# A two-layer mixture kernel: loads held back behind a run-time branch, a single placed inside a pair, and a sort drawn more slowly

## The chip, the core and the metric

The kernel runs on one core of one Trainium2 chip. Time is device time in microseconds (us), the median of three runs. A core has TensorE (PE in the profile; PEld is its weight load), VectorE (DVE), ScalarE (ACT), GpSimd (POOL) and SyncE (SP). SP issues most loads, POOL the stores of results; all transfers run on the core's 16 DMA engines.

## What is computed

Sixteen samples x of 256 tokens by 256 features pass through two layers, each with a residual. In layer 0 each sample goes through one of eight experts, the one with the largest value in `cond_8`; in layer 1 through its two largest, weighted, and through a shared one.

```python
def _L0_cond_ref(x, opcode_onehot, W_up, b_up, W_gate, b_gate, W_down, b_down):
    expert = jnp.argmax(opcode_onehot, axis=-1)
    wu, bu = (W_up[expert], b_up[expert])
    ...
    hidden = jax.nn.silu(up) * gate
    return jnp.einsum('bsh,bdh->bsd', hidden, wd) + bd[:, None, :]

def _L1_cond_ref(x, router_logits, skill_gate, skill_up, skill_down, shared_gate, shared_up, shared_down):
    rw = jax.nn.softmax(router_logits.astype(jnp.float32), axis=-1)
    w, sel = jax.lax.top_k(rw, 2)
    ...
    # out = sum over the two experts of w * (gelu(x @ gate) * (x @ up)) @ down
    return out + _gemma_mlp(x, shared_gate, shared_up, shared_down)

x = x + _L0_cond_ref(x, cond_8, ...)
x = x + _L1_cond_ref(x, cond_8, ...)
```

The hidden width is 512 in layer 0 and 1024 in layer 1. Everything is float32.

## The kernel before

**Units.** Work is cut into units. A `Single` takes one sample through one expert. A `Pair` takes two samples that use the same expert and saves one eighth of the products by Strassen's scheme (Winograd's form): seven block products (`STEPS`) in place of eight. The sums that this needs are made by POOL for the weights (`sums_q`, `sums_d`, lines 411 to 414) and by DVE for the activations (`sums_b`, lines 404 to 406). To find pairs, the kernel sorts the samples by expert at run time: `order_of_work`, once for layer 0 (16 entries) and once for layer 1 (32 entries: sample and expert for both choices). In layer 1 at least 12 pairs exist whatever the input; the remaining eight entries form 0 to 4 more pairs, and what is then left are singles. That number, `more_i`, is known only at run time.

**Quarters.** The hidden dimension of a unit is cut into quarters (two in layer 0, four in layer 1). For each quarter SP loads a block of gate and up weights (`load_q`, line 342, six buffers "q"), and PE does the ups (line 466 for a pair, 613 for a single) into the PSUM banks X, Y and Q. ACT copies X out (447), DVE combines that copy with Y and Q (451), ACT applies the activation (493) and DVE multiplies (494) and makes the sums for the down products. A single has one DVE operation per quarter, 624 in layer 1 and 632 in layer 0. The down weights come by `load_d` (351) into two buffers "d"; the downs (518 for a pair, into A, B and Y; 643 for a single, into Y) give the result, which DVE finishes (540 on ACT, 551), and POOL adds it to the output in HBM (384).

**Order.** Nothing is scheduled by a compiler: the order of instructions on every engine is the order in which the program emits them. `Line` is a hand-made clock. `main` emits a step and moves the clock (two units for a step of a pair, eight for a quarter of a single), and `later` queues a step for a time. So a pair's seven downs stand between the ups of the next unit, from 18 units after the pair's end, one each 6 units. At each quarter `Line.ahead` issues loads five quarters ahead and POOL's sums three ahead. In layer 0 a single can stand among the quarters of a pair (`among`).

**The second sort.** It is a Python generator, `routing`: the softmax, the second choice and the sort of 32 entries, some 45 small DVE operations; the large ones work on 128x1024. `Line.quarter` draws five steps of it at quarters 2 and 3, and one at each later quarter, so its operations stand in DVE's queue between those of the units:

```python
            for _ in range(5 if self.at < 4 else 1):
                next(routing, None)
```

**The branch.** Every engine reads `more_i` (856) and jumps to one of five bodies (`tc.Switch`, 862). In each body stand a shared pair, the singles that are left (`left`), the additional pairs (`more_pairs[:k]`) and two more shared pairs. With this input k is 3: two singles and three pairs. The first instruction of SP in the body is the load of the next quarter:

```python
        left = ones[2 * k :]
        rest = [shared[-NB], *left, *more_pairs[:k], *shared[1 - NB :]]
        quarters[common:] = in_order(rest)[shared[-NB].kp :]
        u, j = quarters[common]
        u.load_q(j)
        run(rest)
```

**Buffers.** `take` hands out the buffers of a ring in turn; "xs" (four of 512 columns) holds a single's samples, "as" (two) its activations in layer 0, "d" (two of 2048 columns) down weights.

Of the kernel before, what the change touches and what calls it, by code (L numbers as in the profile page):

```python
# [1 line left out]

# [5 lines left out]
F32 = mybir.dt.float32  # L8
I32 = mybir.dt.int32
AF = mybir.ActivationFunctionType  # L10
# [4 lines left out]
B, S, D, E = 16, 256, 256, 8  # L15
H0, H1 = 512, 1024
P = 128
KD = D // P
KPS = (H0 // P // 2, H1 // P // 2)
# [7 lines left out]
NB = 3  # L27
N2 = 2 * S
# [30 lines left out]
def kernel(  # L59
# [10 lines left out]
    nc = tc.nc  # L70
# [3 lines left out]
    const = ctx.enter_context(tc.tile_pool(name="const", bufs=1))  # L74
# [6 lines left out]

    RINGS = {
        "q": (6, QB), "s": (5, QB), "d": (2, 4 * KPS[1] * P), "ds": (2, 4 * KPS[1] * P),
        "c": (2, 8 * S), "bt": (7, 7 * S), "xt": (2, 7 * S), "xs": (4, KD * S), "cp": (6, N2),
        "as": (2, N2), "dz": (5, S), "ys": (3, 4 * S), "z": (1, 4 * S), "bq": (4, 4),
    }
    BANKS = {"X": 2, "Y": 2, "Q": 2, "A": 1, "B": 1}
    rings = {
        tag: [const.tile([P, width], F32, name=f"{tag}{i}") for i in range(n)]
        for tag, (n, width) in RINGS.items()  # L90
    }
    rings |= {
        tag: [ps.tile([P, N2], F32, name=f"{tag}{i}") for i in range(n)] for tag, n in BANKS.items()
    }
    turns = {tag: list(range(len(ring))) for tag, ring in rings.items()}
    HELD = ("s", "d", "bt", "ys", "cp")

    turns |= {("later", tag): [] for tag in HELD}

    def take(tag, *shape, of=None):  # L100

        i = turns[tag].pop(0)
        if tag not in HELD:
            turns[tag].append(i)
        else:
            assert (tag, of) not in turns
            turns[tag, of] = i
        t = rings[tag][i]
        n = 1
        for d in shape:  # L110
            n *= d
        t = t[:, :n]
        if len(shape) == 1:
            return t
        names = "abcd"[: len(shape)]
        return t.rearrange(
            f"p ({' '.join(names)}) -> p {' '.join(names)}", **dict(zip(names, shape))
        )

    def when_free(tag, f):  # L120

        if turns[tag] and not turns["later", tag]:
            f()
        else:
            turns["later", tag].append(f)

    def give(tag, of):
        turns[tag].append(turns.pop((tag, of)))
        if turns["later", tag]:
            turns["later", tag].pop(0)()  # L130

    def bank(tag):
        return take(tag, N2)
# [21 lines left out]
    num = const.tile([P, NA], F32, name="num")  # L155
# [145 lines left out]
    class Unit:  # L301
# [30 lines left out]
            return v[:, self.at + t : self.at + t + 1]  # L332


        def load_q(self, j, parts=1):
            t = take("q", QB)
            w = (wq0, wq1)[self.layer]
            src = w[bass.ds(self.expert(), 1), j].rearrange("e p f -> (e p) f")
            width = src.shape[1]
            cuts = [0, QW // 2, width] if parts == 2 else [0, width]  # L340
            for lo, hi in zip(cuts, cuts[1:]):
                nc.sync.dma_start(t[:, lo:hi], src[:, lo:hi])
            self.q[j] = t[:, :QW].rearrange("p (m k h) -> p m k h", m=2, k=4)
            self.bq = getattr(self, "bq", {}) | {j: t[:, QW:]}
# [44 lines left out]
                give("ys", self)  # L389

    class Pair(Unit):
        width, last = 2, False


        def sums_x(self):
# [185 lines left out]
        def run(self, line, among):  # L581

            self.start()
            for j in range(self.kp):
                line.quarter(self, j)
                for k in range(6):
                    line.main(UP, lambda j=j, k=k: self.up(j, k))

                line.later(2 * UP, lambda j=j: self.up(j, 6))
                line.later(  # L590
                    3 * UP, lambda j=j: when_free("bt", lambda: self.act(j))
                )
                line.later(6 * UP, lambda j=j: self.act_sums(j))
                for f in among[j] if j < len(among) else ():
                    f()

            first, step = 18, 6 if self.layer else 3
            if self is shared[-2]:
                step = 7
            for k in range(7):  # L600
                line.later(first + step * k, lambda k=k: self.down(k))

    class Single(Unit):
        width = 1

        def up(self, j):

# [29 lines left out]

        def down(self, j):
            if j == 0:
                self.po = bank("A" if self is l0_ones[0] else "Y")  # L640
            for half in range(2):
                for c in range(KD):
                    nc.tensor.matmul(  # L643
                        self.po[:, bass.ts(c, S)],
                        lhsT=self.d[:, 2 * c + half, j, :],
                        rhs=self.acts[j][:, bass.ts(half, S)],
                        start=(j == 0 and half == 0 and c == 0),
                        stop=(j == self.kp - 1 and half == 1),
                        skip_group_check=True,
                    )  # L650
            if self.layer:
                give("cp", (self, j))
            if j < self.kp - 1:
                return
            if self.layer:
                give("d", self)
                ys = take("ys", KD, 1, S, of=self)
                nc.scalar.activation(
                    ys.rearrange("p c t s -> p (c t s)"), self.po, AF.Copy, scale=self.weight(0)
                )  # L660
                self.done(ys)
            else:
                give("s", self)
                for c in range(KD):
                    xv = self.xt[:, c, :]
                    nc.vector.scalar_tensor_tensor(
                        xv, self.po[:, bass.ts(c, S)], self.bd[:, c : c + 1], xv, ALU.add, ALU.add
                    )
                self.done(self.xt.unsqueeze(2))

        def piece(self, line, j):
            line.quarter(self, j)
            if not self.layer:
                self.up(j)
            else:
                line.main(SINGLE_UP, lambda: self.up(j))
            if self.layer:
                line.later(SINGLE_UP, lambda: self.down(j))
# [23 lines left out]
    l0_first = First(next(names), 0, B - 1)  # L702
    l0_pairs = [Pair(next(names), 0, 2 * i) for i in range(NP1)]
    l0_ones = [Single(next(names), 0, 2 * NP1 + i) for i in range(NS1)]
    shared = [Pair(next(names), 1, None, (2 * i, 2 * i + 1)) for i in range(NPR)]
    pairs = [Pair(next(names), 1, 2 * i) for i in range(NP2)]
    more_pairs = [Pair(next(names), 1, 2 * NP2 + 2 * i) for i in range(NS2 // 2)]
# [4 lines left out]
    among = {u: [[] for _ in range(u.kp)] for u in [*units, *more_pairs, *shared]}  # L712
# [6 lines left out]
    def in_order(units):  # L719

        order = []
        for u in units:
            for j in range(u.kp):
                order.append((u, j))
                for p in among[u][j] if u in among else ():
                    one = p.__self__
                    if p == one.ups:
                        order += [(one, i) for i in range(one.kp)]
        return order

    quarters = [(u, j) for u in (l0_first, l0_ones[0]) for j in range(u.kp)]
    quarters += in_order(units)
    Q_AHEAD, S_AHEAD = 5, 3

    class Line:
# [52 lines left out]
        def quarter(self, unit, j):  # L788

            self.at += 1  # L790
            assert quarters[self.at] == (unit, j)
            self.ahead(self.at)
            self.send()
            for _ in range(5 if self.at < 4 else 1):
                next(routing, None)

        def send(self):
# [4 lines left out]
    line = Line()  # L802
# [31 lines left out]
    def run(units):  # L834
        for u in units:
            if u.width == 2:
                u.run(line, among[u])
            else:
                for j in range(u.kp):
                    u.piece(line, j)  # L840

    quarters += in_order(shared[-NB:-NB + 1])
    run(units)
    for _ in routing:
        pass
# [16 lines left out]
    for k in tc.Switch(which, NS2 // 2 + 1):  # L862
        for o, d in entry:
            o.clear()
            o.update({n: v.copy() if isinstance(v, (list, dict)) else v for n, v in d.items()})
        left = ones[2 * k :]
        rest = [shared[-NB], *left, *more_pairs[:k], *shared[1 - NB :]]
        quarters[common:] = in_order(rest)[shared[-NB].kp :]
        u, j = quarters[common]
        u.load_q(j)  # L870
        run(rest)
        line.flush(1 << 30)
        line.send()


# [56 lines left out]
```

## Time and profile before

| what | us |
|---|---|
| median of 3 runs | 1071.12 (1071.01 to 1071.39) |
| the profiled execution | 1071.5 |
| its span | 1069.9 |
| PE busy | 1049.1 (98%) |
| DVE busy | 772.9 (72%) |
| POOL busy | 573.8 (54%) |
| ACT busy | 342.2 (32%) |
| DMA | 136.96 MB, mean 128 GB/s |

The page gives busy times, the span in 40 slices, the chain of work that ended last, and the costliest groups of instructions. A busy PE is not a PE at its peak: matmuls are pipelined and their ends are modelled, so gaps of PE are read from the starts of the groups that follow one another. The mean granted clock of TensorE is 0.995 of full speed. The first matmul stands at 1.60 us and a pair's ups begin at 26.10; the branch lies at 774 to 784 us; the two singles run from 821 to 874, and the additional pairs follow them.

### The profile page before, as it was taken

To read this page: it belongs to the slowest core of one execution; us is meant where nothing else is said; L and a number is where in the kernel's file an instruction comes from. 1 tells how busy PE (TensorE), PEld (TensorE's weight loads), DVE (VectorE), ACT (ScalarE), POOL (GpSimd) and SP (SyncE) were. 2 spreads that over 40 slices of the span, in tenths; PEclk is the share of its full clock that TensorE was granted. 3 is DMA by queue.
4 is the path that set the end of the run, shared out by engine and by line. 5 is a ranking of instruction groups with operands and counts; after the bars stand their busy time and mean duration, and the time that the engine had idled before them with its cause. 6 is when DMAs were issued, how large, how long until landed. Compare 5 with 4: busy or idle time off the path is not lost.

```text
span 1069.9 us, 14169 instructions
## 1 busy us (share of the span) xinstructions
PE 1049.1 (98%) x4786; PEld 910.0 (85%) x4786; DVE 772.9 (72%) x1166; ACT 342.2 (32%) x546; POOL 573.8 (54%) x630
## 2 busy tenths in 40 slices
PE   8999999999999999999999999999979999999998
PEld 6788888888888888888888888888868887888887
DVE  7898776677877787778777777877755128777774
ACT  2222233333333333333333333333323113333331
POOL 2554454956664675477556756664620156664520
PEclk9999999999999999999999999999989999999999
DMA  7555565453453355335534552454344364354222
GB/s 253 188 187 205 194 191 165 178 131 95 110 138 110 88 135 138 92 89 138 138 99 99 138 137 85 113 138 114 87 101 113 88 201 126 101 138 117 50 71 42
DMA packets 48854, 136.96 MB, mean 128 GB/s; under 512 B 4994, under 2 KB 17410, under 8 KB 45570
## 3 DMA queue, kind: packets, MB, share of 16 engines
q1 hardware_dynamic: 33666, 115.22, 33.9%
q0 software_dynamic: 14816, 20.45, 11.0%
q8 instruction: 41, 0.67, 0.3%
q14 instruction: 43, 0.35, 0.1%
q10 hardware_dynamic: 288, 0.26, 0.1%
HBM read 114.95 MB, written 20.97 MB: 127 GB/s over the span
## 4 chain that ended last, share of the span: by engine, by line
PE 85%; DVE 9%; issue 3%; ACT 2%; DMA 1%; SPq 0%; DVEq 0%; ACTq 0%
PE X L466 21%; PE Q L466 14%; PE Y L466 14%; PE A L518 11%; PE B L518 8%; PE Y L518 7%; PE Y L643 3%; DVE c L451 3%; PE X L613 3%; PE Q L613 2%; DVE bt L404 1%; DVE bt L494 1%; ACT c L493 1%; PE Y L613 1%; DVE bt L405 1%
## 5 line engine op out<-in xcount | busy, mean ns | idle before, releaser
L447 ACT ACTIVATE cp<-X 128x512 f32<-128x512 f32 x300 | 178.7, 596 | 524.1 <-PE X L466 522.6
L494 DVE TENSOR_TENSOR bt<-c 128x1024 f32<-128x1024 f32 x92 | 135.6, 1474 | 95.6 <-ACT c L493 95.6
L466 PE MATMUL Q<-xt,s 128*128 128x256 f32 x736 | 191.2, 383 | 7.4 <-DVE c L451 7.4
L466 PE MATMUL Y<-xt,q 128*128 128x256 f32 x736 | 190.4, 381 | 2.0 <-DVE c L451 1.8
L466 PE MATMUL X<-xt,s 128*128 128x256 f32 x736 | 191.1, 382 | 0.0
L466 PEld LDWEIGHTS Q<-xt,s 128*128 128x128 f32 x736 | 140.4, 192 | 28.6 <-issue 6.8
L466 PEld LDWEIGHTS Y<-xt,q 128*128 128x128 f32 x736 | 138.5, 190 | 25.6 <-DVE c L451 7.0
L466 PEld LDWEIGHTS X<-xt,s 128*128 128x128 f32 x736 | 140.5, 192 | 21.2 <-issue 1.3
L451 DVE TENSOR_TENSOR c<-cp,Q 128x512 f32<-128x512 f32 x200 | 135.8, 679 | 26.2 <-ACT cp L447 21.3
L411 POOL TENSOR_TENSOR s<-q 128x256 f32<-128x256 f32 x100 | 93.9, 939 | 107.3 <-PE Q L466 63.0
L384 POOL DMA_DIRECT2D out_dram<-ys x46 | 49.0, 1066 | 184.9 <-DVE ys L551 68.8
L451 DVE TENSOR_TENSOR c<-cp,Y 128x512 f32<-128x512 f32 x200 | 135.6, 678 | 16.6 <-PE X L466 8.5
L414 POOL TENSOR_TENSOR s<-s,q 128x256 f32<-128x256 f32 x100 | 77.4, 774 | 113.0 <-PE Q L466 113.0
L493 ACT ACTIVATE c<-c 128x1024 f32<-128x1024 f32 x92 | 96.8, 1052 | 22.3 <-DVE c L451 22.2
L412 POOL TENSOR_TENSOR s<-s,q 128x256 f32<-128x256 f32 x100 | 98.7, 987 | 8.4 <-PE Y L643 0.7
L404 DVE TENSOR_TENSOR bt<-bt 128x512 f32<-128x512 f32 x104 | 101.5, 976 | 1.0 <-DMA bt<-x_dram 0.9
L413 POOL TENSOR_TENSOR s<-q 128x256 f32<-128x256 f32 x100 | 95.9, 959 | 0.0
L466 PE MATMUL X<-xt,q 128*128 128x256 f32 x368 | 94.5, 379 | 0.9 <-issue 0.9
L518 PE MATMUL Y<-bt,d 128*128 128x256 f32 x400 | 95.1, 379 | 0.0
L518 PE MATMUL B<-bt,ds 128*128 128x256 f32 x400 | 95.1, 379 | 0.0
L518 PE MATMUL A<-bt,ds 128*128 128x256 f32 x400 | 95.1, 379 | 0.0
L518 PEld LDWEIGHTS Y<-bt,d 128*128 128x128 f32 x400 | 76.0, 190 | 10.3
(129 smaller groups left out, 1230.9 us busy)
## 6 DMA issues: line engine op xcount, KB each, us to landing
q<-wq_dram SPq DMA_DIRECT2D x100, 512.0 KB, 3.6
d<-wd_dram SPq DMA_DIRECT2D x25, 1024.0 KB, 6.4
out_dram<-ys POOLq DMA_DIRECT2D x54, 256.0 KB, 4.4
xt<-x1d SPq DMA_DIRECT2D x46, 256.0 KB, 4.8
q<-wq_dram SPq DMA_DIRECT2D x22, 514.0 KB, 3.8
s<-wd_dram SPq DMA_DIRECT2D x8, 513.0 KB, 4.8
d<-wd_dram SPq DMA_DIRECT2D x4, 513.0 KB, 5.7
xs<-x_dram SPq DMA_DIRECT2D x8, 256.0 KB, 3.8
```

Source lines behind the costliest of these rows:

```text
L404: tt(t[:, 4:6, :], t[:, 0:3:2, :], t[:, 2:4, :], ALU.subtract)
L411: tt(s("S1"), a("A21"), a("A22"), ALU.add)
L412: tt(s("S2"), s("S1"), a("A11"), ALU.subtract)
L413: tt(s("nS3"), a("A21"), a("A11"), ALU.subtract)
L414: tt(s("nS4"), s("S2"), a("A12"), ALU.subtract)
L447: nc.scalar.activation(t, self.banks["X", j], AF.Copy)
L451: nc.vector.tensor_tensor(self.c[j][:, block].rearrange("p m s -> p (m s)"), self.copies[n, j], self.banks[tag, j], op,)
L466: nc.tensor.matmul(self.banks[tag, j][:, bass.ts(m, S)], lhsT=self.q[j][:, m, A_AT[a], :] if a in A_AT else self.s[j][:, m, S_AT[a], :], r ...
L493: nc.scalar.activation(u, u, AF.Gelu_apprx_tanh)
L494: nc.vector.tensor_tensor(t[:, 0:4, :], u, v, ALU.mult)
L518: nc.tensor.matmul(d, lhsT=src[:, j, :], rhs=self.acts[j][:, B_AT[b], :], start=OPENS[k] and j == 0, stop=j == self.kp - 1, skip_group_che ...
L613: nc.tensor.matmul(dst[:, bass.ts(half, S)], lhsT=self.q[j][:, m, 2 * half + c, :], rhs=self.xt[:, c, :], start=(c == 0), stop=(c == KD - 1),)
```

## The change

Four edits, all in the program that emits instructions:

1. Behind the branch the first load of SP gets `behind=True`: before it, DVE, POOL and ACT each write one element of the buffer that the load fills, so that the load, and all that SP issues after it, waits for the three writes. They are the first instructions of these three engines in the body.
2. The last of the singles behind the branch is not a unit of its own any more: its quarters stand among the quarters of the first additional pair (the `host`), its ups right behind that pair's ups of the same quarter, its downs into bank A; the first single's downs go to bank B. The downs of the shared pair in front of them start 24 units after its end instead of 18. For this a third buffer "d" is made of a new tile `spare`; before the branch the same tile serves as two of the four "xs" and as both "as" buffers, so that no memory is added.
3. The second sort is drawn with five steps at quarter 2 and two at quarter 3, then one at each.
4. `po_bank`, `first` and the handling of a `partial` in `in_order` are what these need.

```diff
-        "c": (2, 8 * S), "bt": (7, 7 * S), "xt": (2, 7 * S), "xs": (4, KD * S), "cp": (6, N2),
-        "as": (2, N2), "dz": (5, S), "ys": (3, 4 * S), "z": (1, 4 * S), "bq": (4, 4),
+        "c": (2, 8 * S), "bt": (7, 7 * S), "xt": (2, 7 * S), "xs": (2, KD * S), "cp": (6, N2),
+        "as": (0, N2), "dz": (5, S), "ys": (3, 4 * S), "z": (1, 4 * S), "bq": (4, 4),
...
+    spare = const.tile([P, 4 * KPS[1] * P], F32, name="spare")
+    for i, (tag, at) in enumerate((("xs", 2), ("xs", 3), ("as", 0), ("as", 1))):
+        rings[tag].insert(at, spare[:, i * N2 : (i + 1) * N2])
+        turns[tag].append(at)
+    rings["d"].append(spare)
...
-        def load_q(self, j, parts=1):
+        def load_q(self, j, parts=1, behind=False):
+
             t = take("q", QB)
+            if behind:
+                nc.vector.memset(t[:1, 0:1], 0.0)
+                nc.gpsimd.memset(t[:1, 1:2], 0.0)
+                nc.scalar.activation(t[:1, 2:3], num[:1, :1], AF.Copy)
...
-            first, step = 18, 6 if self.layer else 3
+            first, step = self.first, 6 if self.layer else 3
...
-                self.po = bank("A" if self is l0_ones[0] else "Y")
+                self.po = bank(self.po_bank)
...
-        def piece(self, line, j):
+        def piece(self, line, j, among=False):
             line.quarter(self, j)
-            if not self.layer:
+            if among or not self.layer:
                 self.up(j)
...
-            for _ in range(5 if self.at < 4 else 1):
+            for _ in range({2: 5, 3: 2}.get(self.at, 1)):
                 next(routing, None)
...
-        rest = [shared[-NB], *left, *more_pairs[:k], *shared[1 - NB :]]
+        rest = [shared[-NB], *left[:-1], *more_pairs[:k], *shared[1 - NB :]]
+        turns["xs"], turns["d"] = [0, 1], [*turns["d"], 2]
+        if left:
+
+            host = rest[len(left)]
+            for j in range(host.kp):
+                among[host][j].append(partial(left[-1].piece, line, j, among=True))
+            left[-1].po_bank, left[0].po_bank = "A", "B"
+            shared[-NB].first = 24
         quarters[common:] = in_order(rest)[shared[-NB].kp :]
         u, j = quarters[common]
-        u.load_q(j)
+        u.load_q(j, behind=True)
```

More of the change, by code (lines that the diff above doesn't have):

```diff
@@ L1 @@
 from contextlib import ExitStack
+from functools import partial
 import concourse.bass as bass
@@ L391 @@
     class Pair(Unit):
-        width, last = 2, False
+        width, last, first = 2, False, 18
         def sums_x(self):
@@ L603 @@
     class Single(Unit):
-        width = 1
+        width, po_bank = 1, "Y"
         def up(self, j):
@@ L704 @@
     l0_ones = [Single(next(names), 0, 2 * NP1 + i) for i in range(NS1)]
+    l0_ones[0].po_bank = "A"
     shared = [Pair(next(names), 1, None, (2 * i, 2 * i + 1)) for i in range(NPR)]
@@ L725, in in_order @@
                 for p in among[u][j] if u in among else ():
-                    one = p.__self__
-                    if p == one.ups:
+                    one = p.func.__self__ if isinstance(p, partial) else p.__self__
+                    if isinstance(p, partial):
+                        order.append((one, p.args[1]))
+                    elif p == one.ups:
                         order += [(one, i) for i in range(one.kp)]
@@ L873 @@
         line.send()
+        for a in among[rest[len(left)]]:
+            a.clear()
 def kernel(**inputs):
```

## The prediction

> **What bounds the kernel now.** The page comes first: TensorE is busy 98% of the span, and the chain that ended last is 85% PE. Time can therefore only come from PE work, which the change leaves as it is, or from PE's gaps. So I listed PE's waits over 0.3 us in the timeline, then read the branch by its source lines, by short windows and by the chain of waits, and last the DVE rows in front of each gap.
>
> First PE's large gaps, in the timeline (start, duration, row, idle before it and its releaser):
> ```profile
> 33.35 1.13 PE L466 MATMUL Y<-bt,q 128*128 128x256 f32 x4 [2.50 <-DVE as L632]
> 55.33 1.13 PE L466 MATMUL Q<-bt,s 128*128 128x256 f32 x4 [0.84 <-DVE c L451]
> ...
> 785.19 1.13 PE L466 MATMUL Y<-xt,q 128*128 128x256 f32 x4 [1.43 <-DVE c L451]
> 790.56 2.04 PE L466 MATMUL Q<-xt,s 128*128 128x256 f32 x4 [4.24 <-DVE c L451]
> 898.47 1.59 PE L466 MATMUL Q<-xt,s 128*128 128x256 f32 x4 [2.00 <-DVE c L451]
> ```
> They lie in three places: the start, the branch, and the first pair behind two singles. Each releaser is DVE. A x4 group costs 0.86 us (steps of the chain), a x8 group 1.73.
>
> The branch, by source lines: when each engine reads the branch's value (L856) and passes the target's hint (L862):
> ```profile
> L856 SPq TENSOR_LOAD <-more_i x1: 275/275/275, 753.7 to 753.7; - x1
> L856 DVEq TENSOR_LOAD <-more_i x1: 543/543/543, 775.5 to 775.5; - x1
> ...
> L862 SPq BRANCH_PREFETCH_HINT  x1: 55/55/55, 757.6 to 757.6; - x1
> L862 POOLq BRANCH_PREFETCH_HINT  x1: 56/56/56, 762.2 to 762.2; - x1
> L862 PEldq BRANCH_PREFETCH_HINT  x1: 50/50/50, 774.7 to 774.7; - x1
> L862 ACTq BRANCH_PREFETCH_HINT  x1: 50/50/50, 774.7 to 774.7; - x1
> L862 DVEq BRANCH_PREFETCH_HINT  x1: 56/56/56, 784.2 to 784.2; - x1
> ```
> With the jumps (L927: SP 754.2, POOL 759.6, PE 770.8, ACT 772.2, DVE 776.7) the fetch takes 3.4, 2.6, 3.9, 2.5 and, for DVE alone, 7.5 us. The chain of waits shows that PE's gap is this delay:
> ```profile
> 776.78 7.45 issue
> 784.23 0.06 DVEq L862
> ...
> 784.45 1.30 DVE c L451 x2
> ...
> 786.86 2.96 DVE bt L494
> 789.82 0.61 DVE c L451
> ...
> 790.56 2.04 PE Q L466 x4
> ```
> The windows give the reason (us, then busy of PE, PEld, DVE, ACT, POOL, then PEclk, DMA share, GB/s): full DMA engines during DVE's fetch, and a lower clock after it.
> ```profile
> 778.00:780.00 2.00, 2.00 (x11) 1.77 (x10) 0.00 (x0) 0.60 (x1) 0.00 (x0) 1.00 0.97 241
> 785.00:797.00 12.00, 7.57 (x20) 5.92 (x21) 9.91 (x11) 2.63 (x4) 7.39 (x5) 0.72 0.33 77
> ```
> The traffic is q (512 KB, issued 772.35), d (1024 KB, 773.98) and one out_dram write (774.71, landed after 9.3 us; median 4.4).
>
> [...] Here 0.72 on average follows 4.24 us idle, but 2.00 us idle at 898 also cost clock (0.89 over 898 to 914) and 2.50 at 33 did not. [...] L209 beside POOL took 1.75 us against 1.22 alone; the reduce L210 beside POOL took 1.22.
>
> **Part A, loads behind the branch.** SP's first q load now waits for tiny writes by DVE, POOL and ACT, each the first instruction behind its own branch. Behind it on SP queue q, then d (now in a third d buffer, so it no longer waits for PE, and it is held by this wait alone), then loads that PE's pace releases later (783.03 on). In the trace they left between 760 and 774; now all leave at about 780. Their readers: L613 on the first q at 820.5; d for POOL's ds (786.97), which PE reads at 843. 2 MB at the 241 GB/s above lands by 790, so 30 us of cover remain; if it were gone, each us late would be a us on PE. The writes themselves fall into ACT's idle 4.03 us before 776.08 and POOL's 6.57 before 774.71; DVE's costs about 0.06 (the small memset L815).
>
> DVE's fetch without q and d: not shown, so bounded by the four other engines, 2.5 to 3.9, and by 7.5 if nothing helps. I take SP's 3.4, since one write still runs. DVE is free at 776.7 + 3.4 = 780.1. Then two combines of 0.6 end 781.4, gelu (ACT L493, 1.06) 782.5, L494 at 1.23 (alone: POOL's ds wait for d) 783.8, combine 784.5. PE without the first gap would ask for that bank at 782.73 + 2 x 0.86 = 784.45. So about 0.3 us of stall stays. Loss before: from 774.88 to 797.04 PE did 11 x 0.86 + 2 x 1.73 = 12.95 us of work in 22.16, so 9.2 lost. **A: -8.9.** With 2.5 us of fetch, and PE's own 0.94 at its branch gone too (q no longer in the way): -10.1. With 5.5 us (the write alone holds it): 2.3 us of stall and about 2 of half clock, -5. With 7.5: 0.
>
> **Part B, the last single among a pair's quarters.** Before, two singles (821 to 874) leave DVE idle (13.77 of 53 us busy), and then a pair runs with no downs between its ups: 24.2 us of PE against, per quarter of 6.04, DVE's four combines, L494 and sums (2.7 + 1.2 to 1.5 + 1.5). [...] PE's loss from 896.31 to 914.09: 2.16 (gap at 898.47) + 1.77 (three groups took 4.36 instead of 2.59) + 0.84 + 0.14 + 0.65 = 5.6. After, each quarter of that pair also has a single's 3.45 + 1.73 us of PE for one more DVE op of 0.69, and the shared pair's downs start at 24 instead of 18 and reach into it. DVE then has some 6.6 us of work in 11.2; the 5.6 go. What comes instead: Q banks alternate and a single takes one too, so the host's four quarters all get the same Q, and each opens it one group (0.86) after the last product of the quarter before. DVE must combine in between: 0.27 (matmul's end to DVE's start, as at 876.74) + 0.68 + 0.05 = 1.0, so 0.14 x 4 = 0.5. The single's d load now stands behind a q that PE releases 9.5 us before its first use; q and d (0.4 us apart, 6.4 landing, one to two more for sharing) need 8 to 9.5: I take 0.3, up to 1.5. **B: -4.8** (-5.6 to -2.5).
>
> **Part C, second sort spread out.** At quarter 3 two steps are drawn instead of five. L208 to L210 (1.22 + 1.75 + 1.22) leave the place in front of L632; L632 then runs at 28.5 and PE goes on at 30.60 (29.74 + 0.86), not 33.35: -2.75. But the steps that follow move by three. In front of the combines at 54 to 55.3, L214 to L216 (2.0, stretched by POOL), L217 to L219 (0.55) and L220, L221 (0.35) give way to L210, L211 and L212 (3 x 1.22 = 3.66): 0.8 later, with hand-overs 0.9, and the 0.84 gap at 55.33 grows by it. From the next pair on, downs stand among the ups; before had heavy steps there (L222 to L228) without a gap. The indices are due far later. **C: -1.8** (-2.8 to 0).
>
> **Other edits.** The spare tile holds two xs and two as buffers before the branch: widths, order and waits before the branch are the same, only DVE's sort steps move. 0.
>
> **Sum.** 8.9 + 4.8 + 1.8 = 15.5 from the profiled execution's 1071.5 (span 1069.9 and 1.6 around it): 1056.0. The runs' median is 1071.12, 0.4 below that execution, so **1055.6**.
>
> **Rivals.** (1) The fetch stays slow: the out_dram write goes on, and 780 to 782 is mostly such packets. A gives 4: 1071.1 - 4 - 4.8 - 1.8 = 1060.5. For it: 9.3 us to landing; against: POOL and ACT fetched in 2.5 beside traffic. (2) The interleaved pair gives its 5.6 back through the Q bank and the late d: 1071.1 - 8.9 - 1.8 = 1060.4. Against: DVE has 4 us of slack per quarter there. (3) Slower: the shared Q bank at the four quarter boundaries. If DVE stands in an L494 stretched to 2.96 and sums (2 or more) when the last product ends, PE waits about 5 us each, 20 in all[...]: 1071.1 - 10.7 - 5.6 + 22 = 1077. It decides from 16.3 / 4 = 4.1 us per boundary; only DVE's order puts that combine before L494, which speaks against it. (4) The wait changes nothing for DVE: A is 0, 1064.5.
>
> **How the numbers follow.** All three parts as summed 0.62; (1) 0.18; (2) 0.08; (4) 0.05; (3) 0.05; around zero 0.02. Low end: A at -10.1 (1.2 more), B and C at their best (0.8 and 1.0), not all together: 1053.4. High end: past (1) and (2) with a little of both, 1061.3. A measurement of this kernel can tell about 0.2% from no change, 2.1 us; faster 0.93, within it 0.02, slower 0.05.
>
> **What would show it.** Right: DVE's hint within 4 us of its jump; SP's q at 780; no PE gap over 0.5 us and clock 1.00 from 774 to 797; PE gaps at the host's boundaries near 0.1; no gap at the first pair's seventh product, one of 1.8 near 53. Wrong: DVE's fetch still 5 us or more (A), gaps over 1 us at Q or at the single's d (B), a gap over 3 us near 53 (C).

## The result, and the profile after

The changed kernel takes 1056.56 us in the median (1055.14 to 1057.02) against 1071.07 of the kernel before in the same runs: a ratio of 0.9864, 95% interval 0.9847 to 0.9882. Two repeats, on chips 10 and 13, gave 0.9864 (0.9849 to 0.9879) and 0.9869 (0.9854 to 0.9885). The profiled execution took 1057.02 us, its span is 1055.4, and the mean granted clock is 0.999. All ratios leave out two slow runs of the experiments on chip 8, one of the kernel before (6346 us) and one of the kernel with the held write (5231 us).

PE's gaps over 0.3 us after 26 us, where the pairs begin, in the timeline of the kernel after (start, duration, row, idle before it and its releaser):

```profile
53.25 1.13 PE L478 MATMUL Q<-bt,s 128*128 128x256 f32 x4 [1.53 <-DVE c L463]
137.65 1.13 PE L478 MATMUL Q<-xt,s 128*128 128x256 f32 x4 [0.39 <-DVE c L463]
773.11 1.10 PE L478 MATMUL X<-xt,q 128*128 128x256 f32 x4 [0.80 <-issue]
784.76 1.10 PE L478 MATMUL Q<-xt,s 128*128 128x256 f32 x4 [1.92 <-DVE c L463]
1040.34 0.70 PE L530 MATMUL A<-bt,spare 128*128 128x256 f32 x2 [0.35 <-DVE bt L506]
```

The gap of 2.50 at 33 is gone, and the one of 0.84 at 55 has become 1.53 at 53. At the branch one gap of 1.92 stands where 1.43 and 4.24 stood. From there to the last unit none over 0.3 is left, also not in the pair that holds the single. Where the time went is read by comparing starts of the same group in both traces (one profile of each kernel):

| part | stretch | measured |
|---|---|---|
| start (C) | the branch's first X group, 774.88 to 773.11, less 0.14 that is PE's own branch (0.94 to 0.80) | -1.6 |
| branch (A) | the Q group behind it, 797.04 to 788.29, less the start's 1.6 | -7.1 |
| the rest (B) | the last unit's first A group, 1054.83 to 1040.34, less both | -5.7 |

The sum, 14.5, is the difference of the spans (1069.9 and 1055.4).

The branch after, by source lines: VectorE's jump (L952) and hint (L877, in the target of the jump), then two other engines' hints. The time from jump to hint is called the fetch here.

```profile
L952 DVEq COMPARE_BRANCH  x1: 60/60/60, 775.1 to 775.1; - x1
...
L877 DVEq BRANCH_PREFETCH_HINT  x1: 56/56/56, 780.1 to 780.1; - x1
...
L877 SPq BRANCH_PREFETCH_HINT  x1: 55/55/55, 756.0 to 756.0; - x1
L877 POOLq BRANCH_PREFETCH_HINT  x1: 56/56/56, 760.2 to 760.2; - x1
```

VectorE's fetch took 5.0 us instead of 7.5. The chain of waits of the kernel after shows that this is still what PE waits for: fetch, two combines, gelu, product, combine.

```profile
775.14 4.95 issue
780.10 0.06 DVEq L877
...
780.38 1.30 DVE c L463 x2
...
782.79 1.22 DVE bt L506
784.02 0.61 DVE c L463
784.63 0.14 issue
784.76 1.10 PE Q L478 x4
```

The windows (us, then busy of PE, PEld, DVE, ACT, POOL, then PEclk, DMA share, GB/s), of the kernel after:

```profile
785.00:797.00 12.00, 12.00 (x57) 10.55 (x57) 9.94 (x15) 3.72 (x6) 6.31 (x4) 1.00 0.67 214
874.00:914.00 40.00, 40.00 (x186) 34.67 (x185) 27.48 (x37) 13.49 (x21) 28.41 (x31) 1.00 0.47 146
```

The second of them, of the kernel before:

```profile
874.00:914.00 40.00, 36.94 (x157) 29.86 (x155) 26.53 (x35) 13.91 (x21) 25.01 (x28) 0.96 0.46 144
```

PE has no idle time in either stretch (the gap of 1.92 ends just ahead of the first), and the clock is full in both; before, the first stretch had a clock of 0.72. The loads that were held (DMA share 0.67 at the branch) now run beside PE's work, and no gap of PE goes back to them; POOL's sums of d did wait for d, until 789.26, and PE reads them from 838 on.

### The profile page after: what moved, and what is told of

It is laid out like the page before. It is cut to its first block, busy times and chain, and to the rows that moved or that the text cites. A ratio compares the mean times of both kernels' runs of the same rounds, so it can differ in the third digit from the quotient of the medians.

```text
span 1055.4 us, 14163 instructions
## 1 busy us (share of the span) xinstructions
PE 1043.8 (99%) x4786; PEld 907.1 (86%) x4786; DVE 771.0 (73%) x1167; ACT 343.1 (33%) x547; POOL 578.8 (55%) x631
## 4 chain that ended last, share of the span: by engine, by line
PE 91%; DVE 6%; issue 1%; ACT 1%; DMA 0%; SPq 0%; DVEq 0%; ACTq 0%
PE X L478 23%; PE Q L478 16%; PE Y L478 16%; PE A L530 12%; PE B L530 8%; PE Y L530 8%; PE X L625 3%; PE Y L655 2%; PE Q L625 2%; DVE c L463 1%; PE A L655 1%; PE Y L625 1%; DVE bt L416 1%; PE B L655 1%; ACT c L505 0%
## 5 line engine op out<-in xcount | busy, mean ns | idle before, releaser
L506 DVE TENSOR_TENSOR bt<-c 128x1024 f32<-128x1024 f32 x92 | 133.0, 1445 | 93.0 <-ACT c L505 93.0
L426 POOL TENSOR_TENSOR s<-s,q 128x256 f32<-128x256 f32 x100 | 79.7, 797 | 104.4 <-PE Q L478 104.4
L416 DVE TENSOR_TENSOR bt<-bt 128x512 f32<-128x512 f32 x104 | 107.0, 1029 | 0.9 <-DMA bt<-x_dram 0.8
L424 POOL TENSOR_TENSOR s<-s,q 128x256 f32<-128x256 f32 x100 | 99.6, 996 | 8.4 <-PE Y L655 0.7
L530 PEld LDWEIGHTS B<-bt,ds 128*128 128x128 f32 x400 | 75.9, 190 | 10.6 <-ACT ys L670 0.3
L530 PEld LDWEIGHTS A<-bt,ds 128*128 128x128 f32 x400 | 76.0, 190 | 10.3
```

The source lines that it names most:

```text
L416: tt(t[:, 4:6, :], t[:, 0:3:2, :], t[:, 2:4, :], ALU.subtract)
L424: tt(s("S2"), s("S1"), a("A11"), ALU.subtract)
L426: tt(s("nS4"), s("S2"), a("A12"), ALU.subtract)
L506: nc.vector.tensor_tensor(t[:, 0:4, :], u, v, ALU.mult)
L530: nc.tensor.matmul(d, lhsT=src[:, j, :], rhs=self.acts[j][:, B_AT[b], :], start=OPENS[k] and j == 0, stop=j == self.kp - 1, skip_group_che ...
```

## The experiments

The theory: three separate gains that add up, with A limited by what VectorE's fetch still costs. The rivals: one part does most of it, the gains are given back, or the third d buffer is the cause. Four kernels ran beside each other in each of three groups; all ratios are to the kernel before on the same chip.

**Each part alone.** The kernel before with the wait only:

```diff
+                nc.vector.memset(t[:1, 0:1], 0.0)
+                nc.gpsimd.memset(t[:1, 1:2], 0.0)
+                nc.scalar.activation(t[:1, 2:3], num[:1, :1], AF.Copy)
...
-        u.load_q(j)
+        u.load_q(j, behind=True)
```

> The kernel before with the wait behind the branch alone (two d buffers, two singles as units, sort as before). Theory (three separate gains that add): 7 us less than before, some 1064.0; VectorE's hint 5 us after its jump in place of 7.5, one PE gap of about 1.9 us where 1.43 and 4.24 stood, granted clock 1.00 from 785 to 797; the 2.00 us gap of the first pair behind the singles stays. Rival (the third d buffer does the work, since it lets d leave when SP comes to it): under 3 us less, the hint still 7 us late. Rival (later loads are paid back at their readers): a new gap at the first single or at the pair's down sums, and under 4 us less.

Measured 0.9936 (0.9921 to 0.9951), 6.9 us less. The fetch took 4.5 us (jump 777.5, hint 782.0) with two d buffers, and the clock from 785 to 797 was 1.00. PE's timeline at the branch and behind the singles:

```profile
786.67 1.10 PE L471 MATMUL Q<-xt,s 128*128 128x256 f32 x4 [1.58 <-DVE c L456]
891.62 1.10 PE L471 MATMUL Q<-xt,s 128*128 128x256 f32 x4 [2.00 <-DVE c L456]
900.69 2.05 PE L471 MATMUL Q<-xt,s 128*128 128x256 f32 x4 [2.50 <-DVE c L456]
```

The theory held, and both rivals fall: the wait does its work without the other edits and without a third d buffer, and no gap appears where the held loads are read. The stretch behind the singles stays bad.

The kernel before with the slower sort only:

```diff
-            for _ in range(5 if self.at < 4 else 1):
+            for _ in range({2: 5, 3: 2}.get(self.at, 1)):
```

> The kernel before with the sort drawn as 5 steps at quarter 2 and 2 at quarter 3, nothing else. Theory: 1.7 us less than before, some 1069.4 (2.8 less at the start, 0.7 given back at the gap near 53, 0.4 near 137). Rival (the branch and the pair behind it absorb a shift of the start): no change.

Measured 0.9982 (0.9975 to 0.9988), 1.9 us less, so a shift of the start is not absorbed. The gap at 33 is gone; the one near 53 is 1.91 us here:

```profile
53.63 1.87 PE L466 MATMUL Q<-bt,s 128*128 128x256 f32 x4 [1.91 <-DVE c L451]
```

The changed kernel without the wait and with the sort as before:

```diff
-            for _ in range({2: 5, 3: 2}.get(self.at, 1)):
+            for _ in range(5 if self.at < 4 else 1):
...
-        u.load_q(j, behind=True)
+        u.load_q(j)
```

> The changed kernel without the wait behind the branch and with the sort as before: the last single inside the pair, the later downs and the third d buffer alone. Theory: 5.7 us less than before, some 1065.4; VectorE's hint still 7 us or more after its jump. Rival (part of what was put down to the single belongs to the wait, or the third d buffer alone helps the fetch): more than 8 us less, or under 4.

Measured 0.9928 (0.9914 to 0.9943), 7.7 us less, which lies between the theory's 5.7 and the rival's 8. PE is busy for all of 874 to 914, as in the changed kernel. The surplus stands at the branch. From the timeline, SP's d load and PE's first gap there:

```profile
771.94 0.48 SPq L363 DMA_DIRECT2D spare<-wd_dram  x1
...
787.74 2.05 PE L478 MATMUL Q<-xt,s 128*128 128x256 f32 x4 [4.15 <-DVE c L463]
```

d left 2 us sooner than before (773.98), and the gap of 1.43 in front of this one is gone. The fetch took 5.6 us (jump 775.8, hint 781.4) instead of 7.5: here the theory, which had it at 7 or more, was wrong. So the third d buffer was tried by itself, in the kernel before (the tile `spare` also takes the place of the xs and as buffers before the branch, as in the changed kernel):

```diff
+    rings["d"].append(spare)
...
+        turns["xs"], turns["d"] = [0, 1], [*turns["d"], 2]
```

> The kernel before with the spare tile as third d buffer behind the branch, nothing else. Theory (d then leaves some 2 us sooner, as in the run with the single alone, and lies less in VectorE's fetch): fetch 5.6 to 6.5 us in place of 7.5, 1 to 2 us less than before, some 1070.3; the gap of 2.00 near 898 stays. Rival (d's place does not matter, the run with the single alone gained its surplus elsewhere): fetch 7 us or more and the time of before.

Measured 0.9988 (0.9980 to 0.9997), 0.9 us less by the medians and 1.3 by the ratio. The fetch took 5.7 us (jump 776.3, hint 782.0), the gap of 1.43 is gone, and the stretch behind the singles is as before (1.99, 0.57, 0.48). The third buffer is a small gain at the branch, which the wait, where it stands, already contains (with the wait the fetch is 4.5 us with two d buffers, 4.4 to 5.0 with three). Without it the single is worth 0.9928 / 0.9988 = 0.9940, about 6.4 us, an estimate from two chips. The product of the three parts, counted once, is 0.9936 x 0.9982 x 0.9940 = 0.9858, within the changed kernel's interval. Within these errors the gains add.

**What holds the fetch.** The changed kernel with POOL's first write behind the branch held as well, by a tiny tile that VectorE writes there and POOL writes before its first store:

```diff
+    mark = const.tile([P, 1], F32, name="mark")
...
                 nc.vector.memset(t[:1, 0:1], 0.0)
+                nc.vector.memset(mark, 0.0)
...
         u.load_q(j, behind=True)
+        line.results.insert(0, lambda: nc.gpsimd.memset(mark, 0.0))
```

> The changed kernel with one more wait: POOL's first write of results behind the branch waits for VectorE's first instruction there, so no data moves while VectorE fetches. Theory (this write, issued at 773.07, holds the fetch at 5.0 us): the fetch falls to 2.5 to 3.7 us as on the other engines, the gap of 1.92 us behind it shrinks to under 0.7, 1.3 to 2.0 us less than the changed kernel, some 1054.8. Rival (5.0 us is what VectorE's fetch costs without data traffic): fetch 5.0, same gap, same time within 0.3 us.

Measured 0.9848 (0.9833 to 0.9864); that interval alone does not part it from the changed kernel, the trace does. VectorE's jump and hint, by source lines:

```profile
L955 DVEq COMPARE_BRANCH  x1: 60/60/60, 775.0 to 775.0; - x1
L879 DVEq BRANCH_PREFETCH_HINT  x1: 61/61/61, 778.7 to 778.7; - x1
```

POOL's write and PE's gap, in the timeline of the same kernel:

```profile
780.01 1.09 POOL L398 DMA_DIRECT2D out_dram<-ys  x1 [0.88 <-issue]
...
783.35 1.10 PE L480 MATMUL Q<-xt,s 128*128 128x256 f32 x4 [0.51 <-DVE c L465]
```

The fetch took 3.7 us, about as on SP (3.5) and PE (3.7) in the changed kernel, and the gap fell from 1.92 to 0.51; the group stands 1.41 us earlier. The theory held for the fetch and the gap: the one write of 256 KB cost 1.3 us of fetch between these two profiles. Over all profiles with that write alone in flight the fetch is 4.3 to 5.0 us, and 3.5 to 3.7 without it (table below); from these, an estimate of its cost is about 1 us.

The changed kernel with the three writes on the d buffer, in `load_d`, so that the q loads go when their buffers come free:

```diff
-            if behind:
-                nc.vector.memset(t[:1, 0:1], 0.0)
...
+            if getattr(self, 'behind', False):
+                nc.vector.memset(t[:1, 0:1], 0.0)
...
+        shared[-NB].behind = True
```

> The changed kernel with the three writes on the d buffer instead of the q buffer: the two q loads go when their buffers come free, only d and what follows it wait. Theory ([...]the q load of 512 KB issued near 771 is mostly landed at 775): fetch 5.0 to 5.5 us, within 0.5 us of the changed kernel. Rival (d alone held the fetch): fetch 5.0 exactly as with both held. Rival (q does the harm): fetch 6 us or more and 2 us slower than the changed kernel.

Measured 0.9860 (0.9845 to 0.9875), the time of the changed kernel. VectorE's hint by its source line:

```profile
L877 DVEq BRANCH_PREFETCH_HINT  x1: 56/56/56, 779.5 to 779.5; - x1
```

SP's loads in the timeline of the same kernel:

```profile
770.78 0.33 SPq L350 DMA_DIRECT2D q<-wq_dram  x1
779.79 0.34 SPq L363 DMA_DIRECT2D spare<-wd_dram  x1
```

With the jump at 775.1 the fetch is 4.4 us, no longer than with q held too (5.0, 4.6 and 4.4 in three profiles of the changed kernel). q landed 3.7 us after its issue, at 774.5, before the fetch began. So a q that goes at its own time does no harm here, against the theory's 5.0 to 5.5 us, and the rival that d alone matters fits: what lengthened the fetch from some 4.5 to 7.5 us was d, 1 MB issued 1.6 us behind q. The write was in flight in both cases; no run has d without it.

**The single.** In the changed kernel the downs of the shared pair start later and the first single sums in bank B. Both taken back:

```diff
-            left[-1].po_bank, left[0].po_bank = "A", "B"
-            shared[-NB].first = 24
+            left[-1].po_bank = "A"
```

> The changed kernel with the downs of the shared pair at 18 units as before and the first single's downs in bank Y: the last single still stands among the pair's quarters, but no downs of the shared pair reach into them. Theory (the single's own TensorE work between the pair's ups gives VectorE its slack): no gap over 0.5 us from 850 to 930, within 0.7 us of the changed kernel. Rival (the delayed downs are needed for it): gaps of 1 us or more at Q in that stretch and 2 to 5 us slower than the changed kernel.

Here the pair's ups write into the bank in which the first single's sum is still open, so that single's output is a different one; the instructions and their sizes are the same. Measured 0.9867 (0.9852 to 0.9882), beside 0.9869 for the changed kernel in the same group. The windows of this kernel over the pair:

```profile
850.00:875.00 25.00, 25.00 (x116) 21.52 (x115) 12.61 (x15) 6.55 (x10) 14.21 (x15) 1.00 0.52 147
875.00:900.00 25.00, 25.00 (x116) 21.52 (x115) 16.93 (x24) 8.07 (x13) 15.17 (x20) 1.00 0.47 154
```

PE is never idle, and the time is the same, so the delay and the banks gain no time. But the expectation had one thing wrong: downs of the shared pair do reach into this pair (838.50 to 889.98), four of the seven, as against five in the changed kernel. The last two of them in PE's timeline:

```profile
854.03 1.89 PE L530 MATMUL Y<-bt,spare 128*128 128x256 f32 x8
861.13 1.89 PE L530 MATMUL B<-bt,ds 128*128 128x256 f32 x8
```

In the pair's last two quarters, from 867.17, no down of the shared pair stands, and PE is busy throughout: there the single's own work between the ups is enough. Whether it would be in the first two quarters is not shown.

**The sort.** The changed kernel with no step drawn at quarters 6, 7 and 8:

```diff
-            for _ in range({2: 5, 3: 2}.get(self.at, 1)):
+            for _ in range({2: 5, 3: 2, 6: 0, 7: 0, 8: 0}.get(self.at, 1)):
```

> The changed kernel with no step of the sort at quarters 6, 7 and 8, so that the three large operations in front of the combines at 52 stand later. Theory (they make the gap of 1.53 us near 53): that gap shrinks to under 0.5, no new gap over 0.5 where they stand now, 1.2 to 1.5 us less than the changed kernel. Rival (POOL's contention makes VectorE late there, not the sort): gap as before, no gain. Rival (the steps only move the gap): a new gap of about 1.5 between 60 and 140.

> The changed kernel as it is, beside its variants on one chip: 0.986 of before, some 1056.5, with the gaps of 1.53 us near 53 and 1.92 us near 785.

Measured 0.9857 (0.9841 to 0.9874) against 0.9864 for the changed kernel: not told apart. The gap near 53 is gone, and a new one over 0.5 stands in PE's timeline:

```profile
191.03 1.13 PE L478 MATMUL Q<-xt,s 128*128 128x256 f32 x4 [1.11 <-DVE c L463]
```

The last rival held in kind, only later than it said: the sort ends three quarters later, and its last two large steps now fall between a pair's and a single's operations there.

With both edits, the held write and the sort:

> The changed kernel with both: no sort steps at quarters 6 to 8, and POOL's first write behind the branch held for VectorE. If the gains add: 1.2 from the held write and 1.2 to 1.5 from the sort, so 2.4 to 2.7 us less than the changed kernel, some 1053.9, and faster than both kernels of the case.

Measured 0.9846 (0.9832 to 0.9859), runs of 1054.91 to 1055.44 against 1057.14 to 1057.46 for the changed kernel beside it: 1.9 us less, short of the 2.4 expected, which fits the gap near 190 (1.13 us) that takes the place of the one near 53 (1.34 in the changed kernel beside it). VectorE in front of it, in the timeline:

```profile
186.65 1.21 DVE L236 TENSOR_REDUCE wsort<-ys 128x32 f32<-128x1024 f32 x1
187.77 0.86 DVE L646 SCALAR_TENSOR_TENSOR spare<-Y,q,cp 128x256 f32<-128x256 f32 x2
188.56 0.17 DVE L252 TENSOR_SCALAR nwsort<-wsort 128x32 f32<-128x32 f32 x1
188.64 0.68 DVE L465 TENSOR_TENSOR c<-cp,Y 128x512 f32<-128x512 f32 x1
189.24 0.68 DVE L465 TENSOR_TENSOR c<-cp,Q 128x512 f32<-128x512 f32 x1
```

The reduce of 1.21 us is about as long as the gap. To get it out of there, three small steps were drawn together at quarter 12 and two at quarter 18 (`12: 3, 18: 2` added to the map):

> As the kernel with both edits (the write held, no sort steps at quarters 6 to 8), with three steps drawn at quarter 12 and two at quarter 18, so that the sort's last large steps leave the place in front of the gap of 1.13 us near 190. Theory: that gap goes, no other over 0.6 us before the branch, 3 us less than the changed kernel, some 1053.9. Rival (another gap opens where the drawn steps stand, 75 or 125 to 140): under 2 us less.

> The changed kernel again, beside the next three on one chip: 0.986 of before, some 1057.

Measured 0.9850 (0.9837 to 0.9864), 1054.32 to 1055.68 against 1056.03 to 1056.88 for the changed kernel: 2.0 us less, where the theory had 3. The gap near 190 went with the reduce, and the rival's new one came at 79.70 (0.79 us). VectorE before it:

```profile
75.48 0.75 DVE L224 CAST odd<-ri 128x32 f32<-128x32 int32 x1
76.15 0.18 DVE L225 TENSOR_TENSOR count<-count,rank 128x32 f32<-128x32 f32 x1
76.36 0.69 DVE L226 TENSOR_TENSOR count<-count,odd 128x32 f32<-128x32 f32 x1
77.09 0.64 DVE L227 TENSOR_SCALAR count<-count 128x32 f32<-128x32 f32 x1
```

POOL makes a pair's weight sums from 75.47 to 78.4, and operations that take 0.18 alone take up to 0.75. Both of these kernels are faster than the changed one beside them: no run of theirs is as slow as its fastest, though the intervals of the ratios overlap a little. Between the two the measurement does not decide.

## Why the prediction was right

The likeliest case came true, with each of its three parts, and the result is 1.0 us above the predicted median. That it came so close is in part luck: A fell short by 1.8 us, and half of that was made up by B, which gave 0.9 more than predicted.

**A, -8.9 predicted, -7.1 measured.** The direction is as predicted: with q and d held, VectorE's fetch is shorter (5.0 us for 7.5), SP's loads leave at 780.6, the clock stays full (1.00 from 785 to 797), and no reader on PE is late. The mis-sized term is the fetch, taken as SP's 3.4 us. It was 5.0, so VectorE came 1.6 us later and the stall left over was 1.92 instead of 0.3. By the prediction's own signs this part was not right: the hint did not come within 4 us, a gap over 0.5 stayed, and 5 us is the mark that it had set for being wrong. The prediction named the cause itself: one write still runs. But it put the write's hold into a second case (a fetch of 5.5, A worth 5) and left it out of the main sum; the measured fetch lies between the two. The run with the write held shows the price, and fits the rest of the sum: a fetch of 3.7 left a stall of 0.51, where the working gives 0.3 + 0.3. The second case also counted some 2 us of lost clock, the author's estimate; in the kernel before, the granted clock is 0.50 from 790.5 to 795, behind the gap of 4.24, and 0.62 from 898 to 902, behind the one of 2.00. The stall of 1.92 cost none (1.00 from 785 to 788), but one of 1.91 near 53 did in the kernel with the slower sort alone (the group behind it took 1.87 us, against 1.13 in the changed kernel), so that was not certain.

**B, -4.8 predicted, -5.7 measured.** The cause held: a pair without other work between its ups leaves VectorE too little time per quarter, and a single's 5.2 us of TensorE work there gives it enough. Several terms were off. The 5.6 us of loss missed small delays of 0.07 to 0.14 in the pair's first three quarters (eight between 880 and 894 of before, 0.76 in all). The late d, 0.3, did not come. The shared Q bank did cost what was taken, about: at each of the pair's four boundaries the Q group starts 0.08 and the group behind it 0.11 later than the groups before them last, 0.8 in all against 0.5. A wait of the same kind at 844.49, 0.2 in all, was not foreseen; there a down of the shared pair follows the first single in bank B, and with that single's sum in bank Y it is absent. 5.6 + 0.8 - 0.8 - 0.2 = 5.4, 0.3 short of what the starts show. The delay of the shared pair's downs was counted as a help and is not one: without it the time is the same. What the four downs that reach into the pair anyway are worth is open.

**C, -1.8 predicted, -1.6 measured.** -2.8 at the first pair as worked out; 0.7 given back at 53 where 0.9 was taken; 0.4 more at 137.65, which was not foreseen and did not appear in the two repeats.

**The rivals.** The fetch stayed slow, but not so slow as in rival 1 (A worth 4), which had the right cause. Rival 2 (the single gives its gain back) and rival 3 (PE waits some 5 us at each of the four boundaries, 20 in all; the other 2 of its 22 are the author's estimate of lost clock) fall with the 0.19 us measured at each. Rival 4 (the wait changes nothing) falls with the wait alone, -6.9.

The reasoning behind A, that data in flight lengthen the fetch, pointed the right way. The profiles show how long the fetch took beside which data, not how the one delays the other. VectorE's fetch followed the data in flight:

| data in flight when VectorE jumps | d issued, before the jump | fetch, us |
|---|---|---|
| write and d, the kernel before | 2.7 | 7.5 |
| write and d, slower sort alone | 2.7 | 6.8 |
| write and d, third d buffer alone; single alone | 3.9; 3.9 | 5.7; 5.6 |
| write alone: changed kernel three times, wait alone, d held, single plain, sort later | | 5.0, 4.6, 4.4; 4.5; 4.4; 4.3; 4.7 |
| nothing: write held; both edits; the last version | | 3.7; 3.5; 3.6 |

## What to carry to other kernels

Behind a run-time branch, look at each engine's time from jump to hint: where it is longer on one engine (here 7.5 us on VectorE against 2.5 to 3.9 on the others), see which transfers are in flight there, and hold those that have slack, stores too (3.5 to 3.7 us with all of them held). Where one engine has too little time between the products of a unit, setting unrelated work of the busy engine between them helped here (5.7 us). When steps off the path are spread over time, look at the queue at each place they land in: here moving them late enough to clear one gap (1.53 us near 53) opened another (1.11 at 191, then 0.79 at 80).

## What the runs showed that was not expected

- Part of the fetch is not explained by traffic: with no data in flight it still took 3.5 to 3.7 us on VectorE (three profiles). In the changed kernel the DMA share is 0.95 from 775 to 777 and 0.03 from 777 to 779, and yet the hint comes at 780.1; so some 3 us of it come after the data.
- What an idle stretch costs in clock is not set by its length alone. At 33 us the same gap of 2.50 was followed by a group of 1.13 us in the kernel before and of 1.86 in the one with the wait alone, which is the same program up to the branch; the clock granted from 33 to 36 was 1.00 and 0.60. 1.91 us idle near 53 in the one with the slower sort alone was followed by a group of 1.87, and 1.92 at the branch of the changed kernel by one of 1.10. PE's timeline with the wait alone:

```profile
33.34 1.86 PE L471 MATMUL Y<-bt,q 128*128 128x256 f32 x4 [2.50 <-DVE as L637]
```

- VectorE's smallest operations grew most in proportion beside POOL: from 0.17 to 0.19 us alone for 128x32 to 0.60 to 0.75 for four of the six that stand between 75.4 and 78.4 in the last version (the other two took 0.18 there). The product of 128x1024 grew from 1.22 to 2.96 at most in the kernel before (at 786.86, beside POOL's sums of d at 786.97 and 788.81).
